# Logits from stacked 12-bit halves of queries and keys, passed through DRAM (blocks 0 and 3)

## The chip, the cores and the metric

The kernel runs on one core of a Trainium2 chip. The metric is the device time in microseconds of one execution. Five engines work side by side, each through its own instructions in order: TensorE (PE for its matmuls, PEld for its weight loads), VectorE (DVE), ScalarE (ACT), GpSimd (POOL) and SyncE (SP), which here does nothing but issue DMAs. Engines wait for each other through semaphores.

## The reference

Four transformer blocks run one after the other on x (4 batches, 1024 tokens, 288 channels). Blocks 0 and 3 are alike; their self-attention is what the change touches. In the reference:

```python
h = layer_norm(x, ln1_g, ln1_b, 1e-06)
q8, s, sm = quant_act(h)                       # whole levels from -127 to 127, a scale per token
q = quant_linear(q8, s, sm, wq1, bq1).reshape(b, n, H, D)
k = quant_linear(q8, s, sm, wk1, bk1).reshape(b, n, H, D)
v = quant_linear(q8, s, sm, wv1, bv1).reshape(b, n, H, D)
a = attn(q, k, v)                              # softmax(q k^T / sqrt(D)) v, in f32
a8, sa, sma = quant_act(a)
x = x + quant_linear(a8, sa, sma, wo1, bo1)
```

with 16 heads of D = 18, so that each of the 64 pairs of a batch and a head has a 1024 x 1024 table of logits. The result is rounded to levels again right behind the attention, which is why the logits are computed in f32.

## The kernel before

The file plans all four blocks for one core; `quant_self` (L1891) emits the self-attention of blocks 0 and 3. Heads are padded to 32 rows (HP), so that four heads fill the 128 partitions; there are four groups g of four heads (NG), four batches b, two halves qh of the queries (512 each) and eight tiles kt of 128 keys (NTB).

- The main loop (L2118 to L2154) runs over b, g, qh, kt: 256 steps a block. For this document, the 16 steps of one (b, g) are a turn. A step makes the logits of four heads (L2139: a product per head, keys as weights, 512 queries moving, each head in its own 32 rows of the array), two exponentials on ACT of two heads each (L2149), and the weighing of the values of the step before (`weigh`, L2095), which sums over kt in one bank of PSUM. At the end of a half turn the sums are copied (L2106) and turned to tokens (`heads_done`).
- Besides, each step advances one piece of side work (`step`, L2071): a list `side` of generators, and when that is empty a piece of `spare`. `operands(b, g)` (L1996) makes the queries and keys of the next turn in four pieces, one per operand and half of the tokens: three bf16 matmuls (L2007), a scaling by two factors from PSUM (L2014) and the bias (L2018), into one tile of 128 x 1024 for queries and one for keys, which the logits read directly. It is put at the head of the list, and so stands in the first four steps of a turn. `levels(b)` makes the rounded input of a batch, `values(b)` its values, in eight pieces (L1976), `output` the output projection. levels and values of the next batch are queued together at g = 1, and before g = 3 what is left is emitted in one go (L2126).
- `spare` is `beside`: weights and context of the next stages are prepared there. `level_pieces` (L1609) loads a weight's rows into a tile `wn` (three buffers, loads two chunks ahead), turns them into levels and writes some of them to DRAM (L1701); `ctx_aside` (L1714) uses the same buffers and a context tile that holds every key position twice.
- A scheduler places each engine's instructions from this program; the pools' buffers (`at`, two of each tag unless stated) limit how far anything runs ahead. Of PSUM, three double banks hold logits and two single banks (`ps1`) the sums and all side products. SP's queue takes loads and stores in its own order, each behind the waits of those before it.

The product of an f32 matmul takes two instructions here; the element type F32R, which the change uses, is the one in which line 2644 (`products`, block 2) multiplies values that have been split into two parts of 12 bits.

The lines that the change touches are L1628 to L1639, L1722, L1754 and L1781 (buffers and context), L1821, L1930, L1976 to L1994 (`values`), L1996 to L2022 (`operands`), L2097, L2131 and L2134 to L2145.

Of the kernel before, what the change touches and what calls it, by code (L numbers as in the profile page):

```python
# [37 lines left out]
P = 128  # L38
# [1142 lines left out]
class Fast(Net):  # L1181
# [427 lines left out]
    def level_pieces(self, np_, wd, n_in, width, p, put, sw, bias=None):  # L1609
# [16 lines left out]
        def load(c0):  # L1626
            m = min(per, oc - c0)
            wn = np_.tile([P, 1152], F32, tag="wn", name="wn", bufs=3)  # L1628
# [4 lines left out]
        loaded = [load(c0) for c0 in range(0, oc, per)[:2]]  # L1633
        yield IDLE
        yield
        for c0 in range(0, oc, per):
            m, wn = loaded.pop(0)
            if c0 + 2 * per < oc:
                loaded.append(load(c0 + 2 * per))  # L1639
# [74 lines left out]
    def ctx_aside(self, w, ctxT, mask, cw, np_):  # L1714
# [7 lines left out]
        ctx = self.load_ctx(np_, ctxT)  # L1722
# [30 lines left out]
        def keys_of(g):  # L1753
            wk = np_.tile([P, 1152], F32, tag="wn", name="wn", bufs=3)  # L1754
# [21 lines left out]
        for g in range(NG):  # L1776
# [3 lines left out]
            else:  # L1780
                wv = np_.tile([P, 1152], F32, tag="wn", name="wn", bufs=3)  # L1781
# [34 lines left out]
        for b in range(B):  # L1816
# [4 lines left out]
            self.mm(ps[:, :C], ctx[:, :, b].rearrange("p c r k -> p c (r k)"), wv, 0, C)  # L1821
# [69 lines left out]
    def quant_self(self, L, w, beside, ready, early):  # L1891
# [5 lines left out]
        with ExitStack() as es:  # L1897
# [32 lines left out]
            at, ep = pool(f"{L}at", 2), pool(f"{L}ep", 5)  # L1930
            ext = wp.tile([P, 2, 2 * B * NG], F32, name="sext")
# [44 lines left out]
            def values(b):  # L1976
                st = state[b]
                v = at.tile([P, NTB, H * (D + 1) + HP - D - 1], F32, tag="v", name="v")
                st["v"] = v
                nc.gpsimd.memset(v[:, :, H * (D + 1) :], 0.0)  # L1980
                vh = v[:, :, : H * (D + 1)].rearrange("p j (h d) -> p j h d", d=D + 1)
                nc.gpsimd.memset(vh[:, :, :, D : D + 1], 1.0)
                for j in range(NTB):
                    ps = self.ps1()
# [7 lines left out]
                        vh[:, j, :, :D], self.heads(y), self.heads(wv["b"]), ALU.add  # L1992
# [3 lines left out]
            def operands(b, g):  # L1996

                st = state[b]
                qk = []
                for k, m in zip("qk", wqk):  # L2000
                    d = at.tile([P, S], F32, tag=f"{k}T", name=f"{k}T")
                    qk.append(d)
                    for hf in range(2):
                        cols = slice(hf * 512, (hf + 1) * 512)
                        ps = self.ps1()
                        for c in range(NC3):
# [102 lines left out]
            def turn_heads():  # L2109
                b, g, qh, o = done.pop()  # L2110
                heads_done(b, g, qh, o)
                if g == NG - 1:
                    side.append(output(b, qh))

            run(levels(0))
            run(operands(0, 0))
            run(values(0))
            for b in range(B):  # L2118
# [1792 lines left out]
```

## Time and profile before

| | |
|---|---|
| three runs | 4742.92 us median (4738.52 to 4750.64) |
| the profiled execution | 4740.6 us, its span 4738.7 us |
| mean granted TensorE clock | 0.88 |
| stage of block 0's self-attention | 85.8 to 798.3 us |
| stage of block 3's self-attention | 3585.9 to 4303.9 us |
| DMA over the span | 135.92 MB in 138592 packets, mean 29 GB/s |

A row of the page's groups names the line, the engine, the operation, what it writes and reads with shapes, the count, then the busy time and the mean length of one, then the idle time of the engine just before and what ended it. The shape 32*128 of a matmul is rows by columns of the array. In the timeline, a line begins with the start and the length in us; consecutive instructions of one kind are merged. Ends of matmuls are modelled, so the distance from start to start says what one costs. Other rows of the stages:

```profile
L2095 PE MATMUL ps<-e,v 128*32 128x512 f32 x4096 | 554.6, 612 | 9.1 <-DVE oT L2106 9.1
L2014 DVE SCALAR_TENSOR_TENSOR qT<-ps,wq1sw,srep 128x512 f32<-128x512 f32 x64 | 48.0, 750 | 46.8 <-PE ps L2007 44.5 <-issue 1.0
L2018 DVE TENSOR_SCALAR kT<-kT,bk 128x512 f32<-128x512 f32 x64 | 30.9, 485 | 1.8
L1991 POOL TENSOR_TENSOR v<-y,wv1b 128x288 f32<-128x288 f32 x64 | 51.5, 810 | 562.0 <-DVE y L1988 562.0
```

### The profile page before, as it was taken

The page shows a single profiled execution, that of the slowest core. Times are in us where ns is not written, and L with a number is a line of the kernel's source. Part 1 is how long each engine was busy: PE and PEld are TensorE (multiplying, and loading weights), DVE is VectorE, ACT ScalarE, POOL GpSimd, SP SyncE. Part 2 cuts the span into 40 slices and gives each one's busy share as a digit, 9 for nine tenths or more (in the row PEclk, how much of TensorE's full clock was granted, in tenths as well). Part 3 has the DMA queues.
Part 4 walks back from the last instruction along what each step waited for, and adds up shares of the span by engine and source line. Part 5 has one row for each costly group of instructions (what it writes and reads, how often), then busy time and mean ns, then how long its engine had stood idle before and what let it go on. Part 6 is the DMA issues. An engine that isn't in the chain of part 4 may idle for free. (4 is left out here: it accounts for less than half of the span.)

```text
span 4738.7 us, 62800 instructions
## 1 busy us (share of the span) xinstructions
PE 4183.4 (88%) x22827; PEld 1737.1 (37%) x22827; DVE 3078.2 (65%) x6940; ACT 2992.6 (63%) x4276; POOL 1153.8 (24%) x1742
## 2 busy tenths in 40 slices
PE   4999998889988789999789987799998999997886
PEld 2223223445566431111123333455552232223444
DVE  8355445786644779999889986545345445446885
ACT  2776776566753259999899974222215766774664
POOL 2001001333210567440023340111101000003453
PEclk9999999889999875555589998899998999998898
DMA  3000002110000321000001014002000000001000
GB/s 88 2 6 22 9 11 61 49 42 6 13 13 17 108 96 42 27 18 0 14 21 29 27 32 140 23 19 43 1 3 17 2 10 25 7 13 38 15 18 19
DMA packets 138592, 135.92 MB, mean 29 GB/s; under 512 B 69404, under 2 KB 116124, under 8 KB 136736
## 3 DMA queue, kind: packets, MB, share of 16 engines
q1 hardware_dynamic: 137072, 128.13, 9.3%
q0 software_dynamic: 1200, 3.69, 0.3%
q8 instruction: 181, 2.97, 0.3%
q14 instruction: 139, 1.14, 0.1%
HBM read 79.92 MB, written 43.47 MB: 26 GB/s over the span
## 5 line engine op out<-in xcount | busy, mean ns | idle before, releaser
L2149 ACT ACTIVATE e<-ps 128x1024 f32<-128x1024 f32 x1024 | 992.6, 1021 | 409.3 <-PE ps L2139 401.5
L2139 PE MATMUL ps<-qT,kT 32*128 32x512 f32 x4096 | 624.2, 647 | 2.7 <-DVE sext L2061 2.7
L3201 DVE TENSOR_REDUCE top<-e 128x2 f32<-128x2048 f32 x256 | 563.6, 2282 | 15.6 <-ACT e L3194 15.4
L2095 PE MATMUL ps<-e,v 128*32 128x512 f32 x4096 | 554.6, 612 | 9.1 <-DVE oT L2106 9.1
L3747 PE MATMUL ps<-qk 32*128 32x512 bf16 x1024 | 501.0, 604 | 40.4 <-ACT e L3194 38.6
L3194 ACT ACTIVATE e<-ps 128x1024 f32<-128x1024 f32 x512 | 522.0, 1192 | 6.5 <-PE ps L3747 3.1
L3796 ACT ACTIVATE e<-ps 128x1024 f32<-128x1024 f32 x512 | 476.7, 1076 | 28.7 <-PE ps L3787 15.3
L3802 DVE TENSOR_SCALAR eb<-e 128x2048 bf16<-128x2048 f32 x256 | 325.3, 1277 | 46.4 <-ACT e L3796 45.1
L1874 POOL TENSOR_TENSOR x<-x,y 128x288 f32<-128x288 f32 x192 | 152.5, 806 | 829.6 <-DVE y L1873 485.5
L2643 PE MATMUL psf<-hT,w 128*128 128x512 f32 x576 | 271.7, 594 | 0.6 <-ACT hT L2634 0.6
L2139 PEld LDWEIGHTS ps<-qT,kT 32*128 32x128 f32 x4096 | 184.7, 184 | 201.0 <-issue 128.0
L3787 PE MATMUL ps<-qk,kz 64*128 64x512 bf16 x1024 | 215.4, 422 | 31.5 <-ACT e L3796 27.3
L2095 PEld LDWEIGHTS ps<-e,v 128*32 128x32 f32 x4096 | 81.3, 108 | 403.6 <-issue 344.4
L3747 PEld LDWEIGHTS <-qk 32*128 32x128 bf16 x1024 | 53.0, 99 | 466.0 <-issue 465.0
L3670 ACT ACTIVATE gl<-psf,bf 128x512 f32<-128x512 f32 x72 | 49.4, 686 | 244.3 <-PE psf L2644 229.4
L3194 ACT ACTIVATION_READ_ACCUMULATOR e<-ps 128x1 f32 x512 | 192.4, 376 | 0.0
L1991 POOL TENSOR_TENSOR v<-y,wv1b 128x288 f32<-128x288 f32 x64 | 51.5, 810 | 562.0 <-DVE y L1988 562.0
L2106 DVE COPY oT<-ps 128x512 f32<-128x512 f32 x64 | 44.2, 690 | 213.5 <-PE ps L2095 213.5
L1489 POOL TENSOR_TENSOR h<-h,g 128x288 f32<-128x288 f32 x112 | 91.4, 817 | 362.1 <-ACT h L1486 359.6
L279 PEld LDWEIGHTS <-qT 98*128 98x128 bf16 (+2 forms) x1344 | 130.6, 103 | 125.0 <-issue 37.3
L3685 PE MATMUL psf<-w,u 128*128 128x288 f32 x576 | 147.3, 410 | 1.2 <-DVE u L3674 1.2
L3674 DVE SCALAR_TENSOR_TENSOR u<-psf,bf,gl 128x512 f32<-128x512 f32 x72 | 53.9, 749 | 144.8 <-PE psf L2644 144.7
(549 smaller groups left out, 7908.9 us busy)
## 6 DMA issues: line engine op xcount, KB each, us to landing
raw<-y SPq DMA_DIRECT2D x32, 432.0 KB
in<-raw SPq DMA_DIRECT2D x30, 432.0 KB
kz<-qk SPq DMA_DIRECT2D x128, 64.0 KB
wn<-in_L_wfc SPq DMA_DIRECT2D x12, 432.0 KB
x<-in_x SPq DMA_DIRECT2D x4, 1152.0 KB
vvo<-vt SPq DMA_DIRECT2D x16, 288.0 KB
vo<-vvo SPq DMA_DIRECT2D x4, 1152.0 KB
qn<-rawq SPq DMA_DIRECT2D x4, 1152.0 KB
```

Source lines behind the costliest of these rows:

```text
L1874: nc.gpsimd.tensor_tensor(self.x[:, t, :], self.x[:, t, :], y, ALU.add)
L2095: nc.tensor.matmul(acc[i * HP : (i + 1) * HP, :], lhsT=st["v"][:, kt, h * (D + 1) : h * (D + 1) + HP], rhs=es_[i // 2][:, i % 2, :], start ...
L2139: nc.tensor.matmul(pss[i // 2][:, i % 2, :], lhsT=self.row_tile(kT, i)[:, kt * P : (kt + 1) * P], rhs=self.row_tile(qT, i)[:, qh * 512 : ( ...
L2149: nc.scalar.activation(e, ps, AF.Exp, scale=SCALE)
L2643: nc.tensor.matmul(o, lhsT=a[:, c, :], rhs=b[:, c, :], start=(c == 0), stop=False)
L3194: nc.scalar.activation(e[:, j, :].rearrange("p (a n) -> p a n", a=2), sc, AF.Exp, scale=rstep, accum_out=sums[:, t, h0 + j : h0 + j + 1],)
L3201: nc.vector.tensor_reduce(top[:, t, h0 : h0 + 2], e, AX.X, ALU.max)
L3685: nc.tensor.matmul(ps[:, :C], lhsT=us[f][:, j * P : (j + 1) * P], rhs=w2[:, f, :], start=(f == 0), stop=(f == nf - 1),)
L3747: self.last = self.nc.tensor.matmul(ps[:, c, :], lhsT=self.row_tile(qT, i)[:, g, qt * P : (qt + 1) * P], rhs=self.row_tile(kT, i)[:, g, c ...
L3787: nc.tensor.matmul(pss[i][:, n, :], lhsT=kz[rows, i, kt * P : (kt + 1) * P], rhs=qT[rows, g, qh * 512 : (qh + 1) * 512], start=True, stop= ...
L3796: nc.scalar.activation(e[:, 2 * n : 2 * n + 2, :], ps, AF.Exp, scale=step)
L3802: nc.vector.tensor_scalar(eb, e, MAGIC, MAGIC, ALU.add, ALU.subtract)
```

## The change

Queries and keys are each split into a high part, rounded to F32R, and the low rest. A head's 18 rows of them are stacked four times in 72 rows: high, low, high, low for queries; high, high, low, low for keys. One product over the 72 rows then sums all four partial products. Moving rows to other partitions is done by DMAs: `operands` writes both parts to a DRAM tile (32 DMAs of 18 rows for each (b, g)), and the main loop fetches stacked queries (once per half turn, a half turn ahead) and stacked keys (once per step, three steps ahead). In the same edit the values get a tile per 128 tokens, `values(b + 1)` moves from g = 1 to the second half of g = 3, `wn` has two buffers with one load ahead, and the context tile holds each position once.

```diff
-            wn = np_.tile([P, 1152], F32, tag="wn", name="wn", bufs=3)
+            wn = np_.tile([P, 1152], F32, tag="wn", name="wn", bufs=2)
...
-        loaded = [load(c0) for c0 in range(0, oc, per)[:2]]
+        loaded = [load(0)]
...
-            if c0 + 2 * per < oc:
-                loaded.append(load(c0 + 2 * per))
+            if c0 + per < oc:
+                loaded.append(load(c0 + per))
...
-        ctx = self.load_ctx(np_, ctxT)
+        ctx = self.load_ctx(np_, ctxT, 1)
...
-            self.mm(ps[:, :C], ctx[:, :, b].rearrange("p c r k -> p c (r k)"), wv, 0, C)
+            for r in range(2):
+                self.mm(ps[r * T : (r + 1) * T, :C], ctx[:, :, b, 0, :], wv, 0, C)
...
+            dp = es.enter_context(
+                tc.tile_pool(name=f"{L}ad", bufs=2, space=bass.MemoryType.DRAM)
+            )
...
-                v = at.tile([P, NTB, H * (D + 1) + HP - D - 1], F32, tag="v", name="v")
+                    v = at.tile([P, H * (D + 1) + HP - D - 1], F32, tag="v", name="v", bufs=10)
+                    st["v"].append(v)
...
                 for k, m in zip("qk", wqk):
-                    d = at.tile([P, S], F32, tag=f"{k}T", name=f"{k}T")
-                    qk.append(d)
+                    d = st[k, g] = dp.tile([4, 4, D, S], F32, tag=f"{k}d", name=f"{k}d")
...
+                        y = at.tile([P, 2, 512], F32, tag="hl", name="hl")
+                        hi, lo, bias = y[:, 0, :], y[:, 1, :], m["b"][:, g : g + 1]
                         nc.vector.scalar_tensor_tensor(
-                            d[:, cols], ps, m["sw"][:, g : g + 1], st["srep"][:, cols],
+                            lo, ps, m["sw"][:, g : g + 1], st["srep"][:, cols],
                             ALU.mult, ALU.mult,
                         )
-                        nc.vector.tensor_scalar(
-                            d[:, cols], d[:, cols], m["b"][:, g : g + 1], None, ALU.add
-                        )
+                        nc.vector.tensor_scalar(hi.bitcast(F32R), lo, bias, None, ALU.add)
+                        nc.vector.scalar_tensor_tensor(lo, lo, bias, hi, ALU.add, ALU.subtract)
+                        for i in range(4):
+                            for n in range(2):
+                                to = slice(2 * n, 2 * n + 2) if k == "q" else slice(n, 4, 2)
+                                nc.sync.dma_start(
+                                    d[i, to, :, cols].rearrange("a r n -> r a n"),
+                                    y[i * HP : i * HP + D],
+                                )
                         yield
-                st["qk", g] = qk
+
+            def fetch_queries(b, g, qh):
+                q = at.tile([4 * D, 4, 512], F32R, tag="qs", name="qs")
+                d = state[b]["q", g][:, :, :, qh * 512 : (qh + 1) * 512]
+                nc.sync.dma_start(q.bitcast(F32), d.rearrange("i a r n -> (a r) i n"))
+                return q
+
+            def fetch_keys(b, g, kt):
+                k = at.tile([4 * D, 4, P], F32R, tag="ks", name="ks", bufs=4)
+                d = state[b]["k", g][:, :, :, kt * P : (kt + 1) * P]
+                nc.sync.dma_start(k.bitcast(F32), d.rearrange("i a r n -> (a r) i n"))
+                return k
...
             run(operands(0, 0))
+            queries = [fetch_queries(*turns.pop(0))]
+            keys_ahead(3)
             run(values(0))
...
-                        side.append(values(b + 1))
...
                     for qh in range(2):
+                        if g == NG - 1 and qh and b + 1 < B:
+                            side.append(values(b + 1))
                         for kt in range(NTB):
+                            if kt == 0:
+                                qs = queries.pop(0)
+                            if kt == 1 and turns:
+                                queries.append(fetch_queries(*turns.pop(0)))
+                            ks = keys.pop(0)
                             pss = [self.ps2() for _ in range(2)]
                             for i in range(4):
                                 nc.tensor.matmul(
-                                    pss[i // 2][:, i % 2, :],
-                                    lhsT=self.row_tile(kT, i)[:, kt * P : (kt + 1) * P],
-                                    rhs=self.row_tile(qT, i)[:, qh * 512 : (qh + 1) * 512],
-                                    start=True,
-                                    stop=True,
+                                    pss[i // 2][:, i % 2, :], lhsT=ks[:, i, :], rhs=qs[:, i, :],
+                                    start=True, stop=True,
                                 )
+                            keys_ahead(1)
```

`turns` and `wanted` list the half turns and the key tiles in the order of the loop; `keys_ahead(n)` issues the next n fetches of keys.

More of the change, by code (lines that the diff above doesn't have):

```diff
@@ L1753, in keys_of @@
         def keys_of(g):
-            wk = np_.tile([P, 1152], F32, tag="wn", name="wn", bufs=3)
+            wk = np_.tile([P, 1152], F32, tag="wn", name="wn", bufs=2)
             wk = wk[:CK, : NC3 * P].rearrange("p (c o) -> p c o", c=NC3)
@@ L1780, in ctx_aside @@
             else:
-                wv = np_.tile([P, 1152], F32, tag="wn", name="wn", bufs=3)
+                wv = np_.tile([P, 1152], F32, tag="wn", name="wn", bufs=2)
                 wv = wv[:CK, : NC3 * C].rearrange("p (c o) -> p c o", c=NC3)
@@ L1977, in values @@
                 st = state[b]
-                v = at.tile([P, NTB, H * (D + 1) + HP - D - 1], F32, tag="v", name="v")
[L1979 to L1982, printed above, removed]
-                for j in range(NTB):
+                st["v"] = []
+                for j in range(NTB):
+                    v = at.tile([P, H * (D + 1) + HP - D - 1], F32, tag="v", name="v", bufs=10)
+                    st["v"].append(v)
+                    nc.gpsimd.memset(v[:, H * (D + 1) :], 0.0)
+                    vh = v[:, : H * (D + 1)].rearrange("p (h d) -> p h d", d=D + 1)
+                    nc.gpsimd.memset(vh[:, :, D : D + 1], 1.0)
                     ps = self.ps1()
@@ L1991, in values @@
                     nc.gpsimd.tensor_tensor(
-                        vh[:, j, :, :D], self.heads(y), self.heads(wv["b"]), ALU.add
+                        vh[:, :, :D], self.heads(y), self.heads(wv["b"]), ALU.add
                     )
@@ L1998, in operands @@
                 st = state[b]
-                qk = []
                 for k, m in zip("qk", wqk):
-                    d = at.tile([P, S], F32, tag=f"{k}T", name=f"{k}T")
-                    qk.append(d)
+                    d = st[k, g] = dp.tile([4, 4, D, S], F32, tag=f"{k}d", name=f"{k}d")
                     for hf in range(2):
@@ L2096, in weigh @@
                         acc[i * HP : (i + 1) * HP, :],
-                        lhsT=st["v"][:, kt, h * (D + 1) : h * (D + 1) + HP],
+                        lhsT=st["v"][kt][:, h * (D + 1) : h * (D + 1) + HP],
                         rhs=es_[i // 2][:, i % 2, :],
@@ L2113, in turn_heads, with keys_ahead @@
                     side.append(output(b, qh))
+            turns = [(b, g, qh) for b in range(B) for g in range(NG) for qh in range(2)]
+            wanted = [(b, g, kt) for b, g, _ in turns for kt in range(NTB)]
+            keys = []
+            def keys_ahead(n):
+                for t in wanted[:n]:
+                    keys.append(fetch_keys(*t))
+                del wanted[:n]
             run(levels(0))
             run(operands(0, 0))
+            queries = [fetch_queries(*turns.pop(0))]
+            keys_ahead(3)
             run(values(0))
@@ L2130, in quant_self @@
                         side.append(levels(b + 1))
-                        side.append(values(b + 1))
                     elif g == 1:
                         side.append(early())
-                    qT, kT = state[b]["qk", g]
                     for qh in range(2):
+                        if g == NG - 1 and qh and b + 1 < B:
+                            side.append(values(b + 1))
                         for kt in range(NTB):
+                            if kt == 0:
[3 more added lines that the diff above has]
+                            ks = keys.pop(0)
                             pss = [self.ps2() for _ in range(2)]
```

## The prediction

> **What bounds the kernel now.** I read the page's engine shares first, then the group rows of the lines that the change touches, then busy time by window over the two self-attention stages, and last the timeline of one step and of the queue of SyncE (SP).
>
> ```profile
> PE 4183.4 (88%) x22827; PEld 1737.1 (37%) x22827; DVE 3078.2 (65%) x6940; ACT 2992.6 (63%) x4276; POOL 1153.8 (24%) x1742
> ...
> L2149 ACT ACTIVATE e<-ps 128x1024 f32<-128x1024 f32 x1024 | 992.6, 1021 | 409.3 <-PE ps L2139 401.5
> L2139 PE MATMUL ps<-qT,kT 32*128 32x512 f32 x4096 | 624.2, 647 | 2.7 <-DVE sext L2061 2.7
> ```
>
> The logits matmuls hardly ever wait, and ACT's exponentials wait 401.5 us for them. By window (from the span's start; the columns are length, then busy us of PE, PEld, DVE, ACT, POOL, the granted clock, the DMA share and GB/s), the stages of blocks 0 and 3 are:
>
> ```profile
> 85.80:798.30 712.50, 685.51 (x4927) 208.54 (x4926) 338.87 (x984) 514.54 (x551) 56.54 (x106) 0.98 0.04 11
> 3585.90:4303.90 718.00, 691.17 (x4954) 211.35 (x4952) 326.21 (x913) 517.03 (x553) 57.53 (x107) 0.98 0.04 11
> ```
>
> PE is busy 96% of both; ACT 72%, DVE 47%, DMA 4%. A stage has 256 steps, so a step takes 2.79 us. One step with a piece of operands(), in the timeline (start, length, then the group):
>
> ```profile
> 401.19 1.14 PE L2139 MATMUL ps<-qT,kT 32*128 32x512 f32 x8
> ...
> 402.26 1.07 PE L2095 MATMUL ps<-e,v 128*32 128x512 f32 x8
> 402.42 1.94 ACT L2149 ACTIVATE e<-ps 128x1024 f32<-128x1024 f32 x2 [0.88 <-PE ps L2139]
> ...
> 403.26 0.82 PE L2007 MATMUL ps<-hT,wq1T 96*128 96x512 bf16 x3
> ```
>
> From start to start: logits 1.07 us, weighing 1.00, projection 0.75 (the next logits start at 404.01). PE sets the step; ACT's floor is 2 x 1.02 = 2.04.
>
> **1. The product (L2139).** Removed: four f32 products, two instructions each, in four row groups: 1.07 us a step. Added: four one-pass products of 72 rows, one after the other. The feed-forward of block 2 has such a product of 128 rows (L2644) behind two f32 ones (L2643):
>
> ```profile
> 3032.42 1.88 PE L2643 MATMUL psf<-hT,w 128*128 128x512 f32 x4
> 3033.74 0.80 PE L2644 MATMUL psf<-hTh,w1h 128*128 128x512 f32 x1
> 3034.37 0.59 PE L2643 MATMUL psf<-hT,w 128*128 128x512 f32 x1
> ```
>
> The period is 3034.37 - 3032.42 = 1.95 us; the four f32 instructions stand 0.429 apart in the records, 1.72, which leaves 0.23 for the one-pass product. Its weight load (190 ns) fits beside it. 4 x 0.234 = 0.94, a gain of 0.13 a step. After the weighing, whose array shape differs, one load may stand open again (0.11), so the gain lies between 0.02 and 0.2, the upper end where a projection precedes the logits. A rule speaks against this part: the Trainium skill (TensorE: Matmul & The Clock Gate, Measured speedup vs the span model) gives 3.07x for four row tiles of K=32. By it four f32 products of four passes would take 16 x 0.216 / 3.07 = 1.12 us and four unpacked passes 0.86, an estimated gain of 0.26; the row gives half of that, and I take 0.1 a step. ACT's 2.04 caps the light steps (2.07 now), and it only counts where PE is still the bound (9 of 16 steps, see 2): 512 x 9/16 x 0.1 = **-30 us**. If all 512 steps kept 0.13: -67.
>
> **2. Operands through DRAM, on SP's queue.** For each pair (b, g), operands() now issues 2 operands x 2 halves x 4 heads x 2 copies = 32 writes of 18 rows; a turn of 16 steps also fetches 16 keys and 2 queries. That is 800 DMAs a block, where SP had nearly nothing to do. The trace has no 18-row write. Its nearest row is the copy of one head's 32 rows, four in sequence, as here; and there are two ends:
>
> ```profile
> L3052 SPq DMA_DIRECT2D kz<-qk x128: 507/541/1684, 1729.3 to 2786.0; - x128
> ...
> L1701 SPq DMA_DIRECT2D w1d<-to x24: 799/818/1001, 607.2 to 4253.0; - x24
> L1701 SPq DMA_DIRECT2D w2d<-to x18: 359/360/407, 758.0 to 4286.8; - x18
> ```
>
> kz (min/median/max ns) runs back to back in 0.633 us from start to start (four from 1729.34, 2.51 us in all). Low end: w2d, 128 rows in pieces, 0.36 + 0.04 gap = 0.40. High end: w1d, also a row count that 16 does not divide (98), 0.82 + 0.04 = 0.86. I take 0.633, for the same shape of source. A fetch has 72 rows x 4 pieces; nearest is ctx<-in_ctxT (96 rows x 4 pieces), 0.62 + 0.04 = 0.66. From issue to the last completion count the trace has 2.6 us for kbdd<-kg (256 KB) and 3.7 from wn's issue at 413.79 to its reader (432 KB); a fetch has 144 KB: 2.6.
>
> SP is in order, and the built order of its instructions is in a usual turn: keys for steps 3 and 4, queries, keys for step 5; then **24 writes** (three halves); keys for step 6; 8 writes; keys for steps 7, 8 and on. Three steps of lead cover 7 us, the burst is longer. From the turn's first logits at 0:
> - first half ready: its bias (L2018) ends 4.2 us after the turn's start (median over 28 turns), plus the added third DVE operation, 0.75 as L2014: 5.0.
> - 24 x 0.633 = 15.2: keys for step 6 are issued at 20.2, landed at 22.8. Before, step 6 began at 17.0.
> - 0.66, then 8 x 0.633 = 5.1: keys for step 7 are issued at 25.9, landed at **28.5**. Before, step 7 began at 19.5.
>
> So a turn is 9.0 us late, and steps 7 to 15 can't catch up, since PE and ACT set them. 15 turns of a block carry operands: 30 x 9.0 = **+270**. With 0.86 the same sum gives 5.0 + 20.6 + 0.7 + 6.9 + 2.6 = 35.8, 16.3 late: +490. With 0.40: the third half waits for the first's buffer (two buffers hl), and step 7's keys land at 22.4, 2.9 late: +87.
>
> Here too a rule says otherwise. The skill (DMA: Bandwidth & Descriptors, Issuing engines are not separate DMA queues) calls the issue time usually small relative to the DMA itself. Its section on why a DMA counts to 16 gives 18 rows nine engines; 4 rows of 2048 B each at this trace's 97 ns make 0.39 us of data. By the rule the data would pace the burst and the turn be some 2.9 late, +87; by the row the issue (0.633) does, +270. I go by the row.
>
> **3. The clock.** In the trace the granted clock falls to 0.50 in the stretch 92 to 103 us, in which PE waited for v, and is back at 1.00 after. A turn would now leave PE idle twice, about 4 us each; I put 2 us a turn for slow steps after it: **+60** (0 to 120).
>
> **4. Start of a stage.** operands(0, 0) has no cover: from 83.3 us (first half done) 32 x 0.633, queries, keys: 106.6. Before, logits began at 85.8, but the first two steps took 16 us for values; steady steps ran from 101.9, as if begun at 96.3. values(0) now lies under the writes. 2 x 10 = **+20** (0 to 40).
>
> **5. The rest.** The third DVE operation of 128 halves, 96 us, lies beside PE on an engine that is 47% busy, apart from the 0.75 above; if DVE were the bound, +96. Its write waits for the buffer of two halves before, whose DMA has landed by then (sum above). v in ten tiles and values(b+1) moved into the last turn of b: the same matmuls, DVE and POOL work (8 x 0.81) in other steps, and two small memsets a tile on POOL, which is 8% busy. wn in two buffers, loaded one chunk ahead instead of two: what waits is L1643, at most 7.8 us before; several steps lie between two chunks: 0 (to +20). ctx once instead of twice: nine DMAs less a block, three matmuls more for each b, under 7 us in all. Late pieces of side work made single steps of 9.4 us before; whether the new order keeps them is open: -30 to +30, taken as 0.
>
> **Sum.** Profiled execution: 4740.6 (span 4738.7, 1.9 around it); the median of the runs shown is 4742.9, 0.05% away. 4740.6 - 30 + 270 + 60 + 20 = **5060 us**, 6.7% slower.
>
> **The rivals.**
> - *SP's issue at 0.86* (w1d's kind): 4740.6 - 30 + 490 + 60 + 36 = 5297. For it: 18 is no multiple of 16, as 98. Against: kz's shape is nearer.
> - *SP keeps up and the shorter product decides: faster.* The place is step 7 of a turn: its keys land in time if 5.0 + 32w + 0.66 + 2.6 is below 19.5, so w below 0.35 us. Then only part 1 counts, with some steps free of the load after a change of shape: -30 to -100, **4680**. For it: isolated DMAs issue in 0.32. Against: none back to back does it under 0.40, and at 0.40 the sum is 4740.6 + 87 - 40 + 20 = 4808.
> - *It isn't one pass*: four passes would be 4 x 0.86 = 3.4 us a step, +2.4 x 512: 5950. L2644 speaks against it.
>
> **Chances.** Forecast 0.52, issue at 0.86 0.22, a cheap issue but still slower (4760 to 4830) 0.09, faster 0.12, no change 0.03, not one pass 0.02. A measurement of this kernel tells about 0.3% (14 us) from no change. Faster 0.12, same 0.03, slower 0.85. The range, from the cheap end of the issue to a little past the dear one, is 4800 to 5340; left out are the faster and equal cases and the far end.
>
> **What would show it.** Right: the logits line waits for the DMA ks, steps 6 and 7 of a turn are long and 8 to 15 are not; writes of hl stand 0.6 apart on SP without a gap; the one-pass product at 0.23 from start to start; clock 0.5 after the gaps; ACT's wait for PE far above 400 us. Wrong: no wait for ks, steps of 2.1 to 2.6 throughout, or writes that issue faster than every 0.35 us; a wait for qs or for a landing in place of the issue; or DVE busy above 80% in the stage.

## The result and the profile after

The kernel after takes 5050.3 us in the median of 4 runs (5029.88 to 5062.96), the kernel before 4745.4 (4738.52 to 4750.64): a ratio of 1.0639, 95% interval 1.0601 to 1.0678. It is **slower by 6.4%**; the forecast was 5060. The profiled execution took 5047.8 us, its span is 5045.8, the mean granted clock 0.844 (0.88 before).

The page of the kernel after, first the engines, then the groups that answer to those shown of before:

```profile
PE 4336.2 (86%) x20827; PEld 1986.5 (39%) x20827; DVE 3177.4 (63%) x7068; ACT 2996.2 (59%) x4276; POOL 1160.4 (23%) x1854
...
L2185 ACT ACTIVATE e<-ps 128x1024 f32<-128x1024 f32 x1024 | 989.3, 1022 | 601.2 <-PE ps L2177 600.5
L2177 PE MATMUL ps<-qs,ks 72*128 72x512 f32 x2048 | 692.4, 466 | 57.1 <-DMA ks<-kd 49.3
```

ACT's wait for logits went from 401.5 to 600.5 us, and the logits now wait for keys (25.7 of the 49.3 us are the first steps of the two stages). By window, from the first logits of a stage to the end of its last step (columns as before):

```profile
129.70:954.70 825.00, 759.12 (x3927) 330.12 (x3927) 353.84 (x924) 519.09 (x553) 55.02 (x139) 0.87 0.46 120
3779.40:4608.80 829.40, 764.04 (x3927) 331.78 (x3927) 353.74 (x924) 519.26 (x553) 54.51 (x139) 0.87 0.45 119
```

ACT's work in a stage is nearly as before (519 us in place of 515 to 517), but the clock is 0.87 in place of 0.98, and DMA rose from 11 to 120 GB/s. The spans differ by 307.1 us: first logits of block 0 start at 129.7 in place of 85.8 (+43.9); that stage takes 825.0 in place of 714.9 (+110); from its end to the first logits of block 3 are 2824.7 in place of 2785.3 (+39, again a stage's start); block 3's stage takes 829.4 in place of 717.3 (+112); the rest +2. **All of the loss lies in the two stages and their starts.**

One turn, whose first logits start at 560.30. The queue of SP in the timeline (start, length from the first to the last issue, what, how many):

```profile
565.36 7.85 SPq L2028 DMA_DIRECT2D qd<-hl  x16
574.19 3.78 SPq L2028 DMA_DIRECT2D kd<-hl  x8
578.07 0.56 SPq L2043 DMA_DIRECT2D ks<-kd  x1
579.80 3.58 SPq L2028 DMA_DIRECT2D kd<-hl  x8
583.48 4.99 SPq L2043 DMA_DIRECT2D ks<-kd  x5
```

and rows of the other engines in the same turn:

```profile
571.00 1.20 DVE L1506 TENSOR_SCALAR a<-a,rso 128x288 f32<-128x288 f32 x4
572.11 0.74 DVE L2019 SCALAR_TENSOR_TENSOR hl<-ps,wk1sw,srep 128x512 f32<-128x512 f32 x1
...
573.04 1.21 PE L2177 MATMUL ps<-qs,ks 72*128 72x512 f32 x4
...
576.85 0.82 PE L2010 MATMUL ps<-hT,wk1T 96*128 96x512 bf16 x3
...
581.16 0.88 PE L279 MATMUL ps<-wo1T,aT 96*128 96x288 bf16 x3 [0.68 <-DVE y L1872]
...
581.66 2.08 PE L2177 MATMUL ps<-qs,ks 72*128 72x512 f32 x4
...
586.83 1.34 PEld L2177 LDWEIGHTS ps<-qs,ks 72*128 72x128 f32 x6 [1.66 <-DMA ks<-kd]
```

Steps 0 to 5 start every 2.1 to 3.2 us; step 6 starts at 581.66, 8.6 us after step 5, and step 7 at 586.83, 5.2 us after that. The 24 writes of three halves (a half is one of the four pieces of operands) begin at 565.36 (5.06 us into the turn). Between the second and the third half SP stands still for 1.0 us (573.21 to 574.19): the third half's first DVE operation starts at 572.11. Here DVE was busy with other work until then (L1506), and the first half's writes had landed at 571.52. In 22 of the 28 turns looked at below it is the landing that comes last, and DVE stands idle for it. Only then comes the key fetch for step 6 (578.07, its last completion count at 581.06), then 8 writes, then the key fetch for step 7 (583.48, landed 586.72). Step 7 waits for its key and nothing else. At step 6 two things end together: the key lands 0.6 us before its use, and PE, meanwhile, is given the fourth piece of operands (576.85) and side work (L279 among it), in an order that the build chose before the run; these end near 581.7. So the profile books few waits on keys: the gap is filled with work that has to wait in turn.

The same over turns 1 to 14 of both stages, as medians from the turn's first logits: the key for step 6 is issued at 17.7 and lands at 20.6, and step 6 begins at 22.3; the key for step 7 is issued at 23.3 and lands at 26.6, and step 7 begins at 27.9. Without writes (e1 below) these steps begin at 16.0 and 18.4. So the key for step 7 comes at least 8.2 us late, whatever else holds that step. **But at step 6 the key is the last thing to come in only 4 of the 28 turns** (by the modelled ends of matmuls). In the others PE is still at work that the build put ahead of these logits, in all 28 turns: the weighings of two steps, the fourth piece, and up to 28 matmuls of side work.

### The profile page after: what moved, and what is told of

Same layout as the page of the kernel before. It is cut to its first block, busy times and chain, and to the rows that moved or that the text cites. A ratio compares the mean times of both kernels' runs of the same rounds, so it can differ in the third digit from the quotient of the medians.

```text
span 5045.8 us, 62050 instructions
## 1 busy us (share of the span) xinstructions
PE 4336.2 (86%) x20827; PEld 1986.5 (39%) x20827; DVE 3177.4 (63%) x7068; ACT 2996.2 (59%) x4276; POOL 1160.4 (23%) x1854
## 5 line engine op out<-in xcount | busy, mean ns | idle before, releaser
L2185 ACT ACTIVATE e<-ps 128x1024 f32<-128x1024 f32 x1024 | 989.3, 1022 | 601.2 <-PE ps L2177 600.5
L2177 PE MATMUL ps<-qs,ks 72*128 72x512 f32 x2048 | 692.4, 466 | 57.1 <-DMA ks<-kd 49.3
L2117 PE MATMUL ps<-e,v 128*32 128x512 f32 x4096 | 660.6, 668 | 16.3 <-ACT e L2185 15.4
L2177 PEld LDWEIGHTS ps<-qs,ks 72*128 72x128 f32 x2048 | 403.6, 214 | 345.0 <-issue 202.9
L2117 PEld LDWEIGHTS ps<-e,v 128*32 128x32 f32 x4096 | 98.1, 112 | 277.6 <-issue 177.8
L3706 ACT ACTIVATE gl<-psf,bf 128x512 f32<-128x512 f32 x72 | 49.3, 685 | 246.6 <-PE psf L2680 229.8
L279 PEld LDWEIGHTS <-qT 98*128 98x128 bf16 (+2 forms) x1344 | 129.9, 103 | 124.8 <-ACT qT L1391 38.2
L2019 DVE SCALAR_TENSOR_TENSOR hl<-ps,wk1sw,srep 128x512 f32<-128x512 f32 x64 | 48.0, 749 | 168.4 <-DMA kd<-hl 55.7
L2679 PEld LDWEIGHTS psf<-hT,w 128*128 128x128 f32 x576 | 107.3, 189 | 103.7 <-issue 95.9
```

The costliest lines, as they stand in the source:

```text
L279: self.nc.tensor.matmul(out, lhsT=lhs[:, k, :], rhs=rhs[:, k, c0:c1], start=(k == 0), stop=(k == kc - 1))
L2117: nc.tensor.matmul(acc[i * HP : (i + 1) * HP, :], lhsT=st["v"][kt][:, h * (D + 1) : h * (D + 1) + HP], rhs=es_[i // 2][:, i % 2, :], start ...
L2177: nc.tensor.matmul(pss[i // 2][:, i % 2, :], lhsT=ks[:, i, :], rhs=qs[:, i, :], start=True, stop=True,)
L2185: nc.scalar.activation(e, ps, AF.Exp, scale=SCALE)
L2679: nc.tensor.matmul(o, lhsT=a[:, c, :], rhs=b[:, c, :], start=(c == 0), stop=False)
```

## The experiments

The theory (A): the writes of the operands hold SP's queue, and the keys for steps 6 and 7 stand behind them. Rivals: the other edits, or the stacked product itself, cost the time; or the data of the writes and their landing do, whatever the queue. One more rival is part of nearly every run: the build orders TensorE's instructions anew for each program. Of the 20827 matmuls, after and e9 have all but 210 in the same places, e1 and e11 all but 46; after and e1 differ in 1406. Lateness is read from the time of steps 0 to 6, the clock from the time that stood at 0.5 in both stages, for all kernels the same way (the means are over turns 1 to 14 of both stages; steps 0-6 end where step 7 begins). These columns are of the profiled execution, which in e9 was the slowest of four (5011.7 us):

| kernel | median us | ratio to before, 95% | steps 0-6, us | steps 7-15, us | us at clock 0.5 | first logits, us |
|---|---|---|---|---|---|---|
| before | 4745.4 | | 19.57 | 25.05 | 55 | 85.8 |
| after | 5050.3 | 1.0601-1.0678 | 28.26 | 24.65 | 429 | 129.7 |
| e1 no writes | 4690.7 | 0.9866-0.9900 | 18.45 | 22.04 | 22 | 130.9 |
| e2 rest alone | 4733.2 | 0.9969-0.9986 | 19.69 | 24.40 | 34 | 86.6 |
| e3 spread | 5441.5 | 1.1439-1.1494 | 23.20 | 37.30 | 354 | 127.2 |
| e4 wide | 5739.1 | 1.2071-1.2115 | 51.69 | 23.79 | 919 | 131.8 |
| e5 fetch on POOL | 5183.0 | 1.0894-1.0939 | 22.30 | 34.70 | 457 | 123.4 |
| e6 writes on POOL | 5201.4 | 1.0939-1.0975 | 22.79 | 34.72 | 509 | 114.1 |
| e7 one copy | 5200.7 | 1.0919-1.0962 | 28.71 | 29.37 | 487 | 113.4 |
| e8 rows outermost | 4832.6 | 1.0154-1.0199 | 22.64 | 23.68 | 111 | 104.3 |
| e9 half columns | 4961.4 | 1.0407-1.0475 | 26.97 | 25.33 | 448 | 112.1 |
| e10 = e8, fetch on POOL | 4764.2 | 1.0015-1.0049 | 20.67 | 22.69 | 106 | 104.5 |
| e11 one copy, rows | 4743.1 | 0.9981-1.0004 | 20.35 | 23.40 | 142 | 99.1 |
| e12 = e11's writes, on POOL | 5244.8 | 1.1027-1.1086 | 26.83 | 33.23 | 719 | 100.9 |

**Without writes.**

```diff
-                        for i in range(4):
+                        for i in range(4 if (b, g) == (0, 0) else 0):
```

> Leaves out: the DRAM writes of all operands except those of the first group of the first batch; every head's logits are made from that group's queries and keys. Products, fetches, projections and the three DVE operations stay. Theory A (the burst of 32 writes holds SP's queue, and the keys for steps 6 and 7 stand behind it): no turn stalls, a turn falls from 52.7 us to about 40 (38 and the lumps of side work), 30 turns x 12.7 = -380: 4670 us (4620 to 4730). Theory B (the stacked product and its fetches are slow by themselves): 4950 or more.

4690.7 us. The same groups and windows of this run:

```profile
L2187 ACT ACTIVATE e<-ps 128x1024 f32<-128x1024 f32 x1024 | 992.1, 1021 | 348.5 <-PE ps L2179 348.3
L2179 PE MATMUL ps<-qs,ks 72*128 72x512 f32 x2048 | 623.8, 426 | 26.3 <-DMA ks<-kd 26.3
```

```profile
130.90:774.00 643.10, 641.78 (x3925) 288.41 (x3926) 352.67 (x924) 517.50 (x553) 54.29 (x139) 1.00 0.37 98
3603.00:4251.30 648.30, 646.10 (x3926) 290.16 (x3927) 352.93 (x924) 517.51 (x553) 54.65 (x139) 0.99 0.35 97
```

A turn takes 40.5 us, PE is busy 100% of the stage, the clock is whole. So the writes, with the order that the build makes for them, cost 360 us; the product and the fetches, which stay and move 97 GB/s, cost nothing, and the new product is a gain. (The build puts the fourth piece of operands two steps earlier here than in after, and one step's weighing, not two, between the logits of steps 5 and 6. How much of the 360 us that order would save by itself wasn't tried: after with TensorE in the program's order is the run that is missing.)

**The other edits alone.** The kernel after, with queries and keys as before:

```diff
-                                    pss[i // 2][:, i % 2, :], lhsT=ks[:, i, :], rhs=qs[:, i, :],
+                                    pss[i // 2][:, i % 2, :], lhsT=self.row_tile(kT, i)[:, kt * P : (kt + 1) * P],
+                                    rhs=self.row_tile(qT, i)[:, qh * 512 : (qh + 1) * 512],
```

> The kernel before with only the other edits (values in tiles and moved, two wn buffers, context once); queries and keys stay in SBUF. Theory A: they cost nothing, 4745 us (4715 to 4775). Rival: the later place of the values and the earlier end of the loads cost part of the loss, 4800 to 4850.

4733.2 us: 0.2% faster. The first rival falls.

**The order on the queue.**

```diff
                         for i in range(4):
                             for n in range(2):
...
+                            if i % 2:
+                                yield
-                        yield
```

> The same writes, four a step over eight steps in place of eight a step over four. Theory A (order on SP): four writes (2.0 us) and a fetch (0.4) fit in a step of 2.3 to 2.6, so no key is late and the half clock behind the gaps goes too: 4720 us (4680 to 4800). Theory B (slow product or fetch) and theory L (the landing of writes and the two hl buffers, whatever the order): 4950 or more.

5441.5 us, far outside. The queue of SP in one turn of this run (its first logits start at 677.37):

```profile
678.93 1.72 SPq L2028 DMA_DIRECT2D qd<-hl  x4
680.75 0.51 SPq L2044 DMA_DIRECT2D ks<-kd  x1
687.33 1.38 SPq L2028 DMA_DIRECT2D qd<-hl  x4
689.11 0.29 SPq L2044 DMA_DIRECT2D ks<-kd  x1
```

From 681.3 to 687.33 SP is free and issues nothing. The write at its head waits for a DVE operation, that for a projection on PE (684.23), and the next key stands behind the write. **A write at the head of the queue whose data isn't ready** holds what follows, even when SP has no issue to make. Yet this is not what made the run slow. The key of 689.11 is for step 6, which begins at 695.68. In all 28 turns every key lands at least 2.2 us before its step, and apart from 1.7 us the profile books waits of logits on keys only at the starts of the stages. So the keys came in time, as theory A wanted; the time goes into the steps behind, most of all 8 and 9 (8.5 and 7.1 us, 2.5 and 2.3 in e1). There the build put the weighing and a chain of side work between the logits, and PE waits in it link by link:

```profile
708.81 0.54 PE L279 MATMUL ps<-wo1T,aT 96*128 96x288 bf16 x3 [0.89 <-ACT aT L1522]
709.96 0.53 PE L279 MATMUL ps<-wo1T,aT 96*128 96x288 bf16 x3 [0.61 <-DVE y L1872]
711.18 0.80 PE L1519 MATMUL ps<-idb,q 128*96 128x128 bf16 x6 [0.70 <-DVE y L1872]
711.74 2.06 PE L2178 MATMUL ps<-qs,ks 72*128 72x512 f32 x4
```

The run removed the late keys and made another order, so its time says nothing on what the late keys cost.

**The same bytes in other shapes.** In e4 a write takes 128 rows of one part, to a DRAM tile of 4 heads x 4 copies x 32 rows; in e8 the DRAM tile is laid out by row, so that the row is the outermost dimension of a write, and the stack takes row before copy:

```diff
-                        for i in range(4):
-                            for n in range(2):
-                                to = slice(2 * n, 2 * n + 2) if k == "q" else slice(n, 4, 2)
+                        for n in range(2):
+                            to = slice(2 * n, 2 * n + 2) if k == "q" else slice(n, 4, 2)
+                            for a in range(2):                                     # e4
+                                nc.sync.dma_start(d[:, to, :, cols][:, a], y[:, a, :])
...
+                            nc.sync.dma_start(                                     # e8
+                                d.rearrange("i r a n -> (i r) a n")[:, to, cols], y
+                            )
```

> Each write takes all 128 rows of one part (heads padded to 32 rows), four writes for a half in place of eight; stacks of 128 rows are fetched in place of 72, so a fetch carries 256 KB in place of 144. If the time of an issue on SP paces the burst, 16 writes a turn in place of 32 halve it (12 x 0.45 = 5.4 us): keys for step 7 land near 18, in time, 4720 to 4800. If the data pace it (288 packets of a half over nine engines at 0.118 us now, 512 over sixteen then, both 3.8 us), the burst keeps its length and the time stays at 5000 to 5080.

> A half is written by two DMAs of 128 rows x 2 parts with the row as the outermost dimension; the stack's rows are taken in another order (row, then copy), so a fetch is again one DMA of 72 rows. Eight writes a turn in place of 32; a half is 512 packets of 2 KB over sixteen engines in place of 288 over nine, the same 32 for each engine. If SP's issues pace the burst: 4700 to 4770. If the data do (about 3.8 us a half): keys for step 7 stay late, 4900 to 5050. In the wide run the outermost dimension was 4 and the data moved at the rate of four engines; here sixteen should be busy.

e4: 5739.1 us; e8: 4832.6. The windows of the bursts, of after, of e4 and of e8 (the last two columns are the busy share of the sixteen DMA engines and GB/s):

```profile
568.00:573.00 5.00, 5.00 (x31) 2.19 (x29) 4.49 (x17) 3.89 (x5) 0.00 (x0) 1.00 0.50 135
```

```profile
824.00:836.00 12.00, 6.16 (x17) 2.43 (x17) 1.99 (x3) 2.12 (x3) 0.00 (x0) 0.57 0.26 102
```

```profile
527.00:531.00 4.00, 4.00 (x28) 1.89 (x21) 2.60 (x8) 2.79 (x4) 0.00 (x0) 1.00 1.02 377
```

Shares of 0.50, 0.26 and 1.02 are about eight, four and sixteen busy engines. The Trainium skill (DMA: Bandwidth & Descriptors, Why a DMA increments its semaphore by 16 and not by 1) says that a DMA uses the largest number up to 16 that divides the slowest dimension of both its sides: 9 for the 18 rows of after, 4 for e4 (4 heads on the DRAM side, though 128 rows on the other), 16 for e8. The windows agree, and so do the counts by which a write's landing is told: ten separate ones in after, five in e4, sixteen in e8. A write of e4, 256 KB, leaves SP 2.4 us behind the one before (the second and third of a half's four), near the 2.6 us that 256 KB take at 102 GB/s: SP waits for its own data. The writes of e8 carry 1.8 times the bytes of after's, and the kernel is 218 us faster. Both expectations of e4 were wrong, because its row count said sixteen engines and its outermost dimension four; e8 fell between its two.

**Data or issue.** The 32 writes and their order as in after, each with half the columns; the build leaves the four pieces of operands where they were:

```diff
-                                    d[i, to, :, cols].rearrange("a r n -> r a n"),
-                                    y[i * HP : i * HP + D],
+                                    d[i, to, :, hf * 256 : (hf + 1) * 256].rearrange("a r n -> r a n"),
+                                    y[i * HP : i * HP + D, :, :256],
```

> Leaves out: half of the tokens' operands. The same 32 writes a turn of 18 rows x 2 parts in the same order, with 256 columns in place of 512; fetches keep their size and take the stored half twice. The built order keeps the four pieces of operands where they were. If data pace the burst (nine engines, four packets of 2 KB each a write, about 0.118 us a packet), a write falls from 0.49 to SP's own 0.35 or so: 24 x 0.36 = 8.6 us, keys for step 7 land near 20 in place of 26.6, the half clock behind the gaps goes: 4740 us (4680 to 4800). If 0.49 is the issue on SP, nothing changes: 5000 to 5080.

4961.4 us, 89 less than after, where 300 less or nothing was expected. The data did pace the writes: within a half they stand 0.376 us apart (mean over all 128 halves), 0.494 in after, and the last write of the first half lands 1.5 us behind its issue in place of 3.0 (medians over 28 turns). So 0.494 was the data, not the issue. But the turn hardly noticed (steps 0 to 6: 26.97 in place of 28.26). SP in one turn (first logits at 554.96):

```profile
560.02 6.23 SPq L2028 DMA_DIRECT2D qd<-hl  x16
568.86 2.84 SPq L2028 DMA_DIRECT2D kd<-hl  x8
571.80 0.29 SPq L2043 DMA_DIRECT2D ks<-kd  x1
573.62 2.83 SPq L2028 DMA_DIRECT2D kd<-hl  x8
576.56 1.92 SPq L2043 DMA_DIRECT2D ks<-kd  x3
```

The 16 writes end 1.6 us sooner, and then SP stands for 2.6 us. In this turn, as in the one shown of after, it is DVE's own work ahead of the third half that takes the time: from the first write to the DVE operation that refills the buffer are 6.76 us here (560.02 to 566.78) and 6.75 there, and the landing came 2.3 us before. Over the 28 turns this round trip of a buffer went from 6.4 us to 4.4 (medians). What did not move is the order. **In all 28 turns of both runs the fourth half waits for its projection on PE, which stands behind step 5; its buffer has been free for 1.9 us in after and for 4.4 in e9.** The key for step 6 lands at 17.2 in place of 20.6, 4.5 us before its step, and never comes last; step 6 begins at 22.0 in place of 22.3, because the same weighings and side work stand ahead of it. So with after's order less data buys little, and most of what held step 6 here is that order. What the same writes cost in another order, and what more hl buffers would do, wasn't tried.

**The queue apart from the writes.** e5 has the fetches on POOL, e6 the writes on POOL; e7 writes each half once and fetches it twice; e10 is e8 with the fetches on POOL.

```diff
-                nc.sync.dma_start(k.bitcast(F32), d.rearrange("i a r n -> (a r) i n"))
+                nc.gpsimd.dma_start(k.bitcast(F32), d.rearrange("i a r n -> (a r) i n"))   # e5, e10 alike; e6: the writes
...
-                            for n in range(2):                                             # e7
-                                to = slice(2 * n, 2 * n + 2) if k == "q" else slice(n, 4, 2)
...
+                for n in range(2):
+                    nc.sync.dma_start(
+                        k[2 * n * D : 2 * (n + 1) * D].bitcast(F32),
+                        d.rearrange("i a r n -> (a r) i n"),
+                    )
```

> Only the queue of the fetches of keys and queries is another: POOL in place of SP. Writes, their sizes and their order stay. Theory A (keys stand behind writes in SP's order): no key is late, as in the run without writes: 4720 us (4690 to 4790). Theory D (the data of the writes fill the DMA engines, and keys wait for them on any queue): 4900 to 5050.

> The other way round: the 32 writes of a turn on POOL, fetches on SP. Theory A: 4720 us (4690 to 4790) if POOL issues a write in about 1 us or less (32 us in a turn of 40); theory D: 4900 to 5050. Much above 1 us an issue, the operands themselves come late: over 5100.

> Each half is written once (four writes of 18 rows, both parts) and the fetch makes the copies: two DMAs for keys, four for queries. A turn has 16 writes in place of 32 with half the data, but 56 DMAs on SP in place of 50. Theory A (a burst of writes ahead of a key): 12 x 0.49 = 5.9, keys for step 6 land at 5.0 + 5.9 + 0.9 + 3.4 = 15.2, for step 7 at 18: in time, 4740 us (4700 to 4800). If the number of DMAs on SP decides, 5000 to 5100.

> The run with rows outermost (eight writes a turn over sixteen engines, which they filled for 11 us), with the fetches on POOL's queue; here the build leaves the four pieces of operands at steps 1, 2, 3 and 5, as without this edit. If keys are late because they stand behind the writes in one queue: 4720 us (4690 to 4760). If they are late because the writes' data fill the engines: no better than 4810 to 4850.

5183.0, 5201.4 and 5200.7 us in e5, e6 and e7: none of the first three did what either theory said, and they don't decide between them. (The time of e6 lies where operands were to come late by slow issues on POOL, but an issue took 0.59 us there, not over 1.) Each edit changed the order in which the build puts TensorE's instructions. In after the four pieces of operands stand behind steps 0, 1, 2 and 5 of a turn; in e5 and e6 behind steps such as 1, 3, 9 and 15, in e7 behind 1, 2, 3 and 11. A turn then stalls elsewhere: in e5 steps 5 to 9 run at 1.5 to 2.8 us in every turn of block 0 that makes operands, writes or not, as A wants, but step 11 takes up to 18 us and step 15 up to 14, in some turns step 3 as well. Behind step 15 the next turn's first keys are waited for (115 us in 25 turns); the last piece they come from is written only 33 to 52 us into the turn (block 0). e10 and e8 come nearest to a pair: the four pieces stay at the same steps (behind 0, 1, 2 and 4). In e10 the key for step 7 lands 14.8 us into the turn in place of 21.2, though the writes are the same: what held the key was the queue. The data of the writes only stretch a fetch, to 4.4 us and more from issue to landing (2.3 in e1). Steps 0 to 6 fall from 22.64 to 20.67, where 18.45 is free of stalls, and the time by 68 us to 4764.2, between the two expectations. But these 2.0 us a turn are not the queue alone: 751 matmuls stand elsewhere, and in e8 the logits of step 7 stand behind two steps' weighings and side work, in e10 behind one step's. The 2.2 us that stay are not late keys, which in e10 land over 5 us before steps 6 and 7 (medians). (The last turn of a stage takes 51 us in e10 and 42 in e8; why is open.)

**Two attempts to beat both.** A half is one write of 128 rows x 2 parts, the fetches make the copies (half the data of e8). In e11 TensorE's instructions also keep the program's order; in e12 they don't, and the writes are on POOL.

```diff
+                        nc.sync.dma_start(d.rearrange("i r a n -> (i r) a n")[:, :, cols], y)   # e12: gpsimd
...
+                for n in range(2):
                     nc.sync.dma_start(
+                        k[2 * n * D : 2 * (n + 1) * D].bitcast(F32),
+                        d.rearrange("i r a n -> (r a) i n"),
+                    )
...
+            es.enter_context(tc.manual_schedule(engines={mybir.EngineType.PE}))               # e11 alone
             run(levels(0))
```

> Meant to beat both: a half is one write of 128 rows x 2 parts (1024 packets of 2 KB a turn in place of 2048), the fetches make the copies (two DMAs for keys, three for queries), and TensorE's instructions are kept in the program's order, so that the four pieces stay in the first four steps. By the data: 1024 packets at 184 a us are 5.6 us, less than the 7 us that three steps of lead cover: no late keys, 4691 as without writes, less about 30 us at the start of each stage: 4630 us (4590 to 4700). If the number of DMAs on SP (42 a turn) or the kept order costs: 4750 or more.

> The writes of the run before (one DMA of 128 rows x 2 parts for a half, 1024 packets a turn, copies made by the fetches), but issued on POOL, so that SP holds no write of operands, and with TensorE's instructions left to the build's own order. If late keys come from two things, the writes' data and a write at the head of SP's queue that waits for its DVE operation, both are gone: turns as without writes (about 40 us), first logits near 100 us instead of 131: 4640 us (4600 to 4700), faster than both kernels. If another limit has taken their place (two hl buffers, the 42 DMAs of a turn on SP, POOL's issue), 4735 or more.

e11: 4743.1 us, the same as before (0.9981 to 1.0004). The window of its first stage (in the second the clock is 0.97):

```profile
99.10:820.50 721.40, 684.91 (x3929) 303.24 (x3930) 367.39 (x1020) 517.95 (x553) 54.03 (x140) 0.93 0.45 131
```

Of its 30 turns 16 take 38 to 42 us, as without writes, and ten take 47 to 60; in one of them (59.5) PE waits in its fixed order, 3.1 us at one place, for a DVE that is busy with weights of the next stage, and the clock halves behind it. Its order on PE is that of e1 but for 46 matmuls, so the two can be compared: with one copy of the writes, steps 0 to 6 take 20.35 us in place of 18.45. Most of the lateness can be removed, then; the gain of the product goes into the long turns and into the starts of the stages (first logits at 99.1, 13 us later than before). e12: 5244.8 us, a miss. Hardly a key is late in it (6.9 us of waits of its logits' matmuls in the whole kernel). TensorE in one turn:

```profile
666.02 0.54 PE L279 MATMUL ps<-wo1T,aT 96*128 96x288 bf16 x3
667.67 0.49 PE L1519 MATMUL ps<-idb,q 128*96 128x128 bf16 x6 [1.11 <-DVE y L1872]
669.06 0.54 PE L279 MATMUL ps<-wo1T,aT 96*128 96x288 bf16 x3 [0.89 <-ACT aT L1522]
670.86 0.40 PE L279 MATMUL ps<-wo1T,aT 96*128 96x288 bf16 x1 [1.26 <-DVE y L1872]
```

The build put a chain of side work (transposes, a copy on ACT, a projection, a DVE operation, in turn) between the logits of steps 3 and 4. PE walks it link by link for 5 us, the clock halves, and the steps after it are slow: 719 us at clock 0.5. Why the build chose this order there isn't settled.

## Why the prediction was right, and where its terms were off

The forecast's mechanism held in its main part: the keys for steps 6 and 7 stand behind the writes on SP and land late, and half clock follows. What it did not see is that the build would reorder PE around them. Its sum is within 0.3% of the result, and that is luck: two of its terms were off by much, in opposite directions. Measured terms, in us of the 307 between the two spans, each against the base that the prediction took (28 turns):

| step of the prediction | predicted | measured |
|---|---|---|
| 1 product, in steps 7 to 15 | -30 | -84 (e1's 22.04 - 25.05 a turn) |
| 2 keys behind the writes | +270 | +243 (28.26 - 19.57 a turn) |
| 3 half clock behind the gaps | +60 | +73 (24.65 - 22.04 a turn) |
| 4 start of a stage, to its third step | +20 | +64 (34.3 and 29.5) |
| first and last turns, rest | 0 | +11 |

Against e1, which has the new product and no stalls, the lateness itself is 275 us (28.26 - 18.45 a turn), and the product's gain over all steps 116 (40.49 - 44.62), of which e2's other edits are 15.

**1, the product.** The size failed, not the direction. The logits alone are as predicted or dearer: 1.21 us from start to start, with 0.23 between the one-pass products. What the working left out is the projection ahead of them. Before:

```profile
511.61 0.82 PE L2007 MATMUL ps<-hT,wq1T 96*128 96x512 bf16 x3
512.37 1.14 PE L2139 MATMUL ps<-qT,kT 32*128 32x512 f32 x8
513.44 1.06 PE L2095 MATMUL ps<-e,v 128*32 128x512 f32 x8
```

and in e1, without stalls:

```profile
505.06 0.82 PE L2012 MATMUL ps<-hT,wq1T 96*128 96x512 bf16 x3
505.53 1.28 PE L2179 MATMUL ps<-qs,ks 72*128 72x512 f32 x4
506.74 1.07 PE L2119 MATMUL ps<-e,v 128*32 128x512 f32 x8
```

Projection to logits takes 0.76 before and 0.47 after, logits to weighing 1.07 and 1.21: 0.15 less for the two, the upper end that the prediction named for this case. It took 0.1 on 9 of 16 steps; the gain came to 3.61 us a turn (44.10 in e2 to 40.49), 0.23 a step. That is close in size to the 0.26 that the skill's rule gave, but not for its reason: the rule speaks of the logits, and from logits to weighing PE takes as long in e1 as in e2 (507.8 and 508.5 us, summed over the 28 turns). The gain, 101 us in all, lies ahead of them: 31 from projection to logits, 38 from other side work to logits, 36 from weighing to side work. The prediction went by a row that had only one such product behind an f32 one of 128 rows. Which change of array shape, or which wait, makes the last two wasn't taken apart.

**2, the queue.** The 9.0 us a turn were 8.7 against before, but the way to it was partly wrong, and the errors cancelled. Right: the first half ready after 5.06 us (5.0), the stalls at steps 6 and 7, the order on SP. Wrong: the writes stand 0.494 apart and not 0.633, since the data on nine engines pace them and not the issue (e9), as the skill's rule had it; and the burst isn't without gaps. SP waits 1.0 us ahead of the third half, in most turns for a buffer whose writes have to land, and 1.2 ahead of the fourth, whose piece the build put behind step 5. And a fetch lands after 3.0 and 3.2 us, not 2.6. So keys for step 7 landed after 26.4 us where 28.5 were predicted, and PE began step 7 some 0.8 us behind the landing (median), which the prediction left out; the new product alone would have begun it at 18.4 and not 19.5. The rule's other half, a turn only 2.9 late, failed: it took 97 ns for a packet of 2 KB, where those of the burst took 127 on average (565.4 to 573.0), so that four make 0.51 us; and it took the fourth half for ready in time.

**3, the clock.** Right in kind; a little small. Half clock came in nearly every turn (429 us of two stages, 55 before), 3.4 to 41 us at a time. The statement that steps 8 to 15 would not be long was wrong: at 0.5 they took 3.7 to 6.3. That all of the 73 us in steps 7 to 15 are the clock isn't shown.

**4, the start.** The term that was off most for its size. It let 32 writes follow each other from 83.3 us. The queue, a window, and one row each of DVE and PE:

```profile
84.54 8.12 SPq L2028 DMA_DIRECT2D qd<-hl  x16
101.90 19.92 SPq L2028 DMA_DIRECT2D kd<-hl  x16
```

```profile
85.00:99.50 14.50, 0.00 (x0) 0.00 (x0) 14.50 (x50) 0.00 (x0) 0.00 (x0) 0.51 0.32 82
99.52 0.75 DVE L2019 SCALAR_TENSOR_TENSOR hl<-ps,wk1sw,srep 128x512 f32<-128x512 f32 x1
...
100.31 0.88 PE L279 MATMUL ps<-wv1T,hT 96*128 96x288 bf16 x3 [16.39 <-DVE hl L2019]
```

SP waits from 92.7 to 101.9 for the third half. It isn't the buffer that is missing: the first half's writes had landed at 90.7. DVE is busy without a pause (14.50 of 14.50 us, 50 instructions) with layer norms, levels and weights that the build put ahead of the third half; the fourth comes at 115.97, 21 us after its buffer was free. PE stands 16.4 us, because the projections of the keys' halves hold both single banks of PSUM, and the values need one. So the step that failed is the assumption that DVE would turn to the halves at once. Why the build ordered DVE so isn't settled. With fewer or smaller writes the first logits come at 104.3 (e8) and 112.1 (e9) in place of 129.7.

**5, the rest** cost nothing, as said (e2: 0.2% faster). But that a half's buffer would have landed by the time it is needed was wrong: in 22 of 28 turns the third half waits for it, and DVE stands idle, 2.0 us a turn on average. A wait for a landing was one of the prediction's signs of being wrong; it came beside the writes' pace, not in its place.

**The rivals.** *Issue at 0.86*: no; the writes are faster than the forecast took them. *SP keeps up*: its condition, a write under 0.35 us, was never met (0.376 even with half the data). Yet e9 shows that it would hardly have been enough in the built order, since the fourth half and the logits of step 6 stand behind other work on PE. *Not one pass*: the products stand 0.23 apart.

## What to carry to other kernels

A detour through DRAM inside a loop is costed by the time at which its data have landed, against the lead of whoever needs them: buffer free, data made, write issued, landed, fetched. Bytes or issues alone don't give it, and anything else on the same in-order queue waits with it. Lay the data out so that the outermost dimension of a transfer, on both sides, is a multiple of sixteen: e8, which does so with fewer and larger writes, is 218 us faster than after. A queue of their own brought the keys in earlier, but whether the kernel gained hung on the order that the build then made (68 us less in e10 against e8, 133 more in e5 against after). Where a scheduler orders the instructions, compare that order before a run is read: an edit of a queue or a size can move work on other engines, and then the run answers another question than the one that was asked. And ask of each late step what came last: a key that is late on the queue costs nothing while PE has other work ahead of its use.

## What the runs showed of the hardware that was not expected

- The number of rows on the SBUF side does not decide a DMA's rate: 128 rows with an outermost dimension of 4 in DRAM moved 102 GB/s, with 128 outermost 377 GB/s, with 18 outermost 135.
- Issues of writes on SP follow each other at 0.32 to 0.38 us; behind four of 72 KB the next two stand 0.65 and 0.67 us apart (medians of first halves of after), and with half the data the step is gone (0.37 throughout, e9). Behind writes of 256 KB at 102 GB/s (e4) an issue takes 2.4 us.
- The last write of a half landed 3.0 us behind its issue in after and 1.5 with half the bytes (e9); a fetch of 144 KB landed after 2.3 us without writes (e1), 3.0 to 3.3 behind after's burst, 4.4 to 4.8 in the runs whose writes moved 377 GB/s (e8, e10).
- A projection of three bf16 matmuls occupies TensorE for 0.47 us ahead of a one-pass 72-row product, and for 0.75 ahead of the four f32 products in row groups (medians; e1 and before).
